# Two layers of a graph network on one core: seven chunks of edges in each layer fetched row by row by SyncE

## The chip, the cores and the metric

The kernel runs on one core of a Trainium2 chip. The metric is the device time of one launch in microseconds (us): three runs of the kernel before took 2022.58 us in the median (2019.66 to 2022.99). The profile is of one more execution, which took 2021.09 us; its span, from the first to the last recorded instruction, is 2019.3 us.

The core's engines are named as in the profile: PE is TensorE's matrix unit and PEld its weight load, DVE is VectorE, ACT is ScalarE, POOL is GpSimd and SP is SyncE, which computes nothing and issues transfers. All transfers, whoever issues them, are carried by the core's 16 DMA engines.

## The reference

There are 6250 nodes with 512 features each and 100000 edges, sorted by destination. Cut to what matters, all in float32:

```python
h = relu(layernorm(x))
norm = -dinv[src] * dinv[dst]              # dinv: degree ** -0.5
prop = lambda v: segment_sum(v[src] * norm[:, None], dst)
h = h @ W1_0 + prop(h) @ W1_1 + b1         # layer 1
h = layer_norm(h, gamma, beta)
h = where(h >= 0, h, 0.01 * h)
out = x + h @ W2_0 + prop(h) @ W2_1 + b2   # layer 2
```

So each layer has two dense products of 6250 x 512 by 512 x 512, and a sum over the edges, for which 100000 rows of 2 KB are read from a table in HBM in the order of `src`.

## The kernel before, in words

*Chunks, units, groups, blocks.* The edges are cut into `NC` = 782 chunks of 128. A chunk is one gather: 128 rows of a table, one in each SBUF partition. Three chunks in a row (`STEP`) form a unit, whose destinations fall into 32 consecutive nodes (`Q`), and four units form a group; there are `NS` = 66 groups in a layer, with up to 12 chunks each. A block is 128 nodes; there are `NB` = 49.

*The gathers.* `gather_to` (L473 to L485) issues them on GpSimd with an indirect DMA each (L480). The rows land in `places`, a tile of 63 places of 528 words per partition: 512 features, and a word D that holds the source's `dinv` in layer 1. Function `slot` (L466) gives a chunk its place. The first chunks fill all 63 places; after that the ring has R = 55 places, and the last eight, R to 62, hold layer 2's weights (`w_late`). GpSimd may run a ring's length ahead of the sums; a gather into a place waits until the sums have read the chunk that lay there. The table of layer 1 (`tab[0]`) has rows of 528 words and that of layer 2 (`tab[1]`) rows of 512. The first 76 chunks (`RAW`) are gathered from x itself before the table is there, and normalized in place (`look_up`, L519). The first 27 chunks of layer 2 are gathered early (`gather_ahead`, L490), before the last three blocks of layer 1 are done; what these lack is added from counts (`count_late`).

*The sums.* For a group, `choose` (L591) makes on VectorE a matrix `sel` of zeros and ones that says which edge belongs to which of the 32 nodes of its unit; in layer 1 `scale` (L635, L647) multiplies it by the word D of the gathered rows, in as few instructions as the places are consecutive. `sums` (L651, L660) multiplies: one matmul for each chunk of the group, 12 in all, unit by unit into 32 rows of `ps`. ScalarE copies the sums to `agg` (L673).

*The dense part.* When all groups of a block are summed, `turn` (L784) collects the block's rows with 0/1 matrices (`place`, L693), and `own`, `first_half`, `second` transpose and multiply by the two weights (L568). `finish` (L746) ends the block. In layer 1 it normalizes and stores the block's rows to layer 2's table (L777) and to `h_tab` (L782); in layer 2 it adds x (L755) and stores the output (L757).

*Order.* The loop over groups (L892) is written out by hand for TensorE, GpSimd and SyncE: they take their instructions in the program's order. VectorE and ScalarE are ordered by a planner. SyncE's queue holds, group by group, the loads of a block's own rows `h` two blocks ahead (L545, two buffers), in layer 2 the loads of x (L564), and the stores. The transfers of SyncE use eight completion semaphores in turn; in the built program a transfer waits for the one eight before it, unless a wait already covers that. Buffers that matter below: `t` has two, `g` one, `xt` two.

*Weights.* W1_1 and W1_0 lie in `w_sb[0]` and `w_sb[1]`, and `w_sb[1]` is last used at the end of layer 1. W2_1 and W2_0 are loaded into `places` in layer 1's group 33 (L896). `pick` and `src_lo` are two small tiles that serve `look_up` and `find` in the first groups and nothing after.

Of the kernel before, what the change touches and what calls it, by code (L numbers as in the profile page):

```python
# [10 lines left out]
BF = mybir.dt.bfloat16  # L11
I32 = mybir.dt.int32
AF = mybir.ActivationFunctionType
OP = mybir.AluOpType
# [11 lines left out]
Q = 32  # L26
# [7 lines left out]
AHEAD_OF = 27  # L34
JOIN = 12


# [6 lines left out]
def gnn_kernel(  # L44
# [85 lines left out]
    sc = const.tile([P, 2, NB], F32, name="sc")  # L130
    pick = const.tile([P, P], BF, name="pick")
    src_lo = const.tile([P, P], BF, name="src_lo")
    src_hi = const.tile([P, RAW], F32, name="src_hi")
# [292 lines left out]
    with tc.If(n_unseen > 0):  # L426
        general_path(tc, x, src, dst, bias1, bias2, gam, bet, w_sb, (W2_1, W2_0), dinv, ndinv, ident, iota_r,
                     eps, out)


def usual_path(tc, have):
    nc = tc.nc
    (x, out, tab, h_tab, ndinv, sidx, dlx, iota_r, w_sb, W2_1, W2_0, w_late, ident, eps, ones, first, nodes_ps, node_of, minus,
     unsorted, dinv, sdinv, bias1, bias2, gam, bet, unseen, unit, N, E, D, NB, NC, NU, NS, KD, rows, places, R,
     load_rest, sc, pick, src_lo, src_hi, eidx, e_src, zero_row, p_id, lent, X) = (
        have[n] for n in ("x out tab h_tab ndinv sidx dlx iota_r w_sb W2_1 W2_0 w_late ident eps ones first nodes_ps node_of "
                          "minus unsorted dinv sdinv bias1 bias2 gam bet unseen unit N E D NB NC NU NS KD rows places "
                          "R load_rest sc pick src_lo src_hi eidx e_src zero_row p_id lent X").split())
    AHEAD = 2
# [11 lines left out]
    with ExitStack() as es:  # L451
# [12 lines left out]
        LATER = places.shape[1] - R  # L464

        def slot(k):  # L466
            return k - X if k < X + R + LATER else (k - X - LATER) % R

        def zr(layer, t):
            k = layer * NC + t  # L470
            return lent[k] if k < X else places[:, slot(k), :D]

        def gather_to(layer, summed_to):  # L473
            nonlocal gathered
            end = summed_to + R
            if layer == 0:
                end = max(end, min(end + LATER, X + LATER + 2 * R))
            for t in range(gathered, min(end, NC)):
                own_scale = layer == 0 and t >= RAW
                nc.gpsimd.indirect_dma_start(  # L480
                    out=places[:, slot(t), :] if own_scale else zr(layer, t), out_offset=None,
                    in_=x if layer == 0 and t < RAW else tab[layer],
                    in_offset=bass.IndirectOffsetOnAxis(
                        ap=lidx[:, t - SHIFTED : t - SHIFTED + 1] if layer and t >= SHIFTED else sidx[:, t : t + 1], axis=0))
            gathered = max(gathered, min(end, NC))  # L485
# [149 lines left out]
        def scale(sel, chunk, of=(0, NQ)):  # L635
# [6 lines left out]
            each = sel.rearrange("p q s e -> p (q s) e")  # L642
            cut = sorted({start, end} | {t for t in range(start + 1, end) if slot(t) != slot(t - 1) + 1})
            for lo, hi in zip(cut, cut[1:]):
                v = each[:, lo - at : hi - at, :]
                k = slot(lo)
                last = nc.vector.tensor_tensor(  # L647
                    v, v, places[:, k : k + hi - lo, D : D + 1].to_broadcast([P, hi - lo, Q]), op=OP.mult)
            return last

        def sums(layer, g, sel, chunk, cnt=None, some=None, opens=True, closes=True):  # L651
# [7 lines left out]
            for s, q in some:  # L659
                nc.tensor.matmul(ps[q * Q : (q + 1) * Q, :], sel[:, q, s, :], zr(layer, chunk[q][s]), start=(s == 0),  # L660
                                 stop=(s == len(chunk[q]) - 1 and (cnt is None or chunk[q][0] >= AHEAD_OF)))
# [224 lines left out]
        for layer in range(2):  # L886
# [5 lines left out]
            for g in range(NS - 1):  # L892
                gather_to(layer, STEP * unit[g])
                if layer == 0 and g == NS // 2:
                    for k, w in enumerate((W2_1, W2_0)):
                        nc.sync.dma_start(w_late[:, k], w.rearrange("(k p) d -> p k d", p=P))  # L896
# [24 lines left out]
                sel, chunk = chosen.pop(g) if g in chosen else choose(g)  # L921
                if layer == 0:
                    with ExitStack() as order:
# [17 lines left out]
                else:  # L941
# [86 lines left out]

def general_path(tc, x, src, dst, bias1, bias2, gam, bet, w_sb, w_late, dinv, ndinv, ident, iota_r, eps,
                 out):  # L1030
# [34 lines left out]
    e_src = dram.tile([NC, P], I32, name="e_src")  # L1065
    e_dst = dram.tile([NC, P], I32, name="e_dst")
    w_sb = list(w_sb)
    for k, w in enumerate(w_late):
# [285 lines left out]
```

## Time and profile before

| | |
|---|---|
| median of three runs | 2022.58 us |
| profiled execution | 2021.09 us |
| its span | 2019.3 us |
| TensorE, matmuls busy | 1669.7 us (83%) |
| GpSimd busy | 1488.9 us (74%) |
| VectorE busy | 707.6 us (35%) |
| ScalarE busy | 414.3 us (21%) |
| mean rate of the DMA engines | 262 GB/s |

A few words on reading it. The slices give the busy share in 40 equal parts of the span, in tenths. A group row has its line, engine, operation and tiles, the count, then busy time and mean duration, then the engine's idle time before these instructions and what ended it. A wait row has the waiting instruction, what released it, the total, the count, and the longest single wait. On GpSimd the recorded duration of a gather is the time in which its descriptors are made, not that in which its data moves; the transfer lands later. "issue" as a releaser means that the engine waited for nothing that the profile shows. SyncE's transfers have their issue time only.

### The profile page before, as it was taken

Reading aid. Unit: us, or ns where it says so; the run is one execution under the profiler, and the core shown is the slowest. Engines: PE = TensorE matmul, PEld = TensorE weight load, DVE = VectorE, ACT = ScalarE, POOL = GpSimd, SP = SyncE. Lnnn points to the kernel's source line nnn. Section 1 sums busy time; section 2 is a strip of 40 time slices with the busy share of each in tenths; the row PEclk is TensorE's granted clock in tenths of the full one; section 3 lists DMA queues with packets and bytes.
Section 4 is the critical chain, followed back from the end, with each engine's and each line's share of the span. In section 5 each row is a group of like instructions: output and inputs, shape, how many; then the busy total and the mean of one; then the engine's idle time right before and its main releaser. Section 6 shows DMA issues by size and latency. Waiting matters only on the chain.

```text
span 2019.3 us, 20097 instructions
## 1 busy us (share of the span) xinstructions
PE 1669.7 (83%) x6907; PEld 669.5 (33%) x6907; DVE 707.6 (35%) x1498; ACT 414.3 (21%) x752; POOL 1488.9 (74%) x1578
## 2 busy tenths in 40 slices
PE   5579998776887776888879888888888888888988
PEld 4444443222333222333323322323332223333333
DVE  7975554333354334343363111112221212222211
ACT  7895221111121111121111010011010001011100
POOL 6477777777777777777777777777777777777774
PEclk8789999888998888989999998889999989989999
DMA  9998888888988888888887787788787878788875
GB/s 329 396 374 269 267 269 263 249 258 245 303 265 253 251 260 241 267 266 260 245 261 241 245 257 247 247 252 255 240 255 246 254 244 257 241 263 251 272 235 171
DMA packets 190131, 528.41 MB, mean 262 GB/s; under 512 B 34652, under 2 KB 36426, under 8 KB 190020
## 3 DMA queue, kind: packets, MB, share of 16 engines
q0 software_dynamic: 125120, 415.88, 67.7%
q1 hardware_dynamic: 64860, 111.14, 15.2%
q8 instruction: 56, 0.92, 0.2%
q14 instruction: 55, 0.45, 0.1%
q10 hardware_dynamic: 40, 0.02, 0.0%
HBM read 475.25 MB, written 51.66 MB: 261 GB/s over the span
## 4 chain that ended last, share of the span: by engine, by line
PE 39%; DMA 31%; POOL 12%; issue 10%; DVE 5%; ACT 2%; POOLq 0%; DVEq 0%; SPq 0%; ACTq 0%
DMA places<-tab,sidx 24%; PE u_ps L568 16%; POOL places L480 12%; PE ps L660 12%; PE an_ps L693 7%; DMA places<-tab,lidx 5%; PE hT_ps L556 1%; PE hT_ps L803 1%; DVE hi L362 1%; DVE lo L362 1%; ACT places L539 1%; DMA dst_c<-in_dst_dram 1%; DMA tab<-places 1%; PE both_ps L379 1%; DVE sel L647 0%
## 5 line engine op out<-in xcount | busy, mean ns | idle before, releaser
L480 POOL DMA_INDIRECT places<-tab,sidx x1191 | 1130.5, 949 | 363.4 <-issue 256.2
L660 PE MATMUL ps<-places,sel 128*32 128x512 f32 x3104 | 517.1, 671 | 145.4 <-DMA places<-tab,sidx 81.9
L693 PE MATMUL an_ps<-agg,there 128*128 128x512 f32 (+1 forms) x554 | 270.0, 620 | 88.2 <-ACT agg L673 83.2
L480 POOL DMA_INDIRECT places<-tab,lidx x270 | 255.3, 946 | 82.3 <-issue 60.9
L660 PEld LDWEIGHTS ps<-places,sel 128*32 128x32 f32 x3104 | 103.1, 117 | 524.1 <-issue 190.0
L607 DVE TENSOR_TENSOR sel<-dlx,nodes_ps 128x384 f32<-128x384 f32 (+3 forms) x134 | 72.4, 541 | 415.1 <-PE ps L660 415.1
L568 PE MATMUL u_ps<-w,hT 128*128 128x512 f32 (+1 forms) x400 | 185.3, 607 | 20.6 <-ACT hT L558 20.1
L673 ACT ACTIVATE agg<-ps 128x512 f32<-128x512 f32 (+2 forms) x130 | 76.1, 587 | 570.1 <-PE ps L660 545.1
L568 PE MATMUL u_ps<-places,hT 128*128 128x512 f32 (+2 forms) x408 | 182.4, 591 | 2.9 <-ACT hT L558 2.9
L568 PE MATMUL u_ps<-w,aT 128*128 128x512 f32 x384 | 173.2, 594 | 2.7 <-DVE aT L805 2.7
L693 PEld LDWEIGHTS an_ps<-agg,there 128*128 128x128 f32 (+1 forms) x554 | 105.8, 199 | 209.6 <-issue 109.8
L568 PE MATMUL u_ps<-places,aT 128*128 128x512 f32 x384 | 173.5, 594 | 0.8 <-DVE aT L805 0.8
L647 DVE TENSOR_TENSOR sel<-sel,places 128x384 f32<-128x384 f32 (+11 forms) x71 | 34.4, 490 | 328.3 <-DMA places<-tab,sidx 323.2
L754 DVE TENSOR_TENSOR u_ps<-u_ps,bias 128x512 f32<-128x512 f32 x45 | 31.5, 700 | 281.8 <-PE u_ps L568 281.8
L558 ACT ACTIVATE hT<-hT_ps 128x512 f32<-128x512 f32 (+1 forms) x98 | 58.2, 594 | 278.1 <-PE hT_ps L556 277.6
L796 ACT ACTIVATE an<-an_ps,ndinv 128x512 f32<-128x512 f32 x96 | 65.8, 685 | 213.7 <-PE an_ps L693 213.5
L681 DVE TENSOR_SCALAR there<-iota_r,node_of 128x128 f32<-128x128 f32 (+1 forms) x286 | 85.8, 302 | 63.6 <-PE an_ps L693 61.3
L568 PEld LDWEIGHTS u_ps<-w,hT 128*128 128x128 f32 (+1 forms) x400 | 73.7, 195 | 96.5 <-issue 74.7
L766 ACT ACTIVATE sd<-mv,eps 128x1 f32<-128x1 f32 (+1 forms) x49 | 14.4, 294 | 433.5 <-DVE mv L764 433.5
L250 POOL DMA_INDIRECT places<-in_x_dram,sidx x63 | 60.0, 952 | 54.0 <-ACT junk L266 21.1
L568 PEld LDWEIGHTS u_ps<-places,hT 128*128 128x128 f32 (+1 forms) x408 | 74.4, 192 | 76.5 <-issue 71.5
L568 PEld LDWEIGHTS u_ps<-w,aT 128*128 128x128 f32 x384 | 70.7, 190 | 83.0 <-issue 77.8
(197 smaller groups left out, 1318.6 us busy)
## 6 DMA issues: line engine op xcount, KB each, us to landing
places<-tab,sidx POOLq DMA_INDIRECT x1191, 3.8
h_tab<-g SPq DMA_DIRECT2D x48, 256.0 KB
xt<-in_x_dram SPq DMA_DIRECT2D x48, 256.0 KB
out_dram<-t SPq DMA_DIRECT2D x48, 256.0 KB
tab<-t SPq DMA_DIRECT2D x46, 256.0 KB
tab<-places SPq DMA_DIRECT2D x22, 528.0 KB
h<-tab SPq DMA_DIRECT2D x45, 256.0 KB
h<-h_tab SPq DMA_DIRECT2D x45, 256.0 KB
```

Source lines behind the costliest of these rows:

```text
L250: nc.gpsimd.indirect_dma_start(out=lent[t] if t < X else places[:, t - X, :D], out_offset=None, in_=x, in_offset=bass.IndirectOffsetOnAxis ...
L362: nc.vector.tensor_tensor(t, s[:, g * 2 * GJ : (g + 1) * 2 * GJ].rearrange("p (j s) -> p j s", s=2)[:, :, None, :] .to_broadcast([EP, GJ, ...
L480: nc.gpsimd.indirect_dma_start(out=places[:, slot(t), :] if own_scale else zr(layer, t), out_offset=None, in_=x if layer == 0 and t < RAW ...
L558: nc.scalar.activation(hT[:, :, :r], ps[:, :, :r], AF.Copy)
L568: nc.tensor.matmul(u_ps[:r], hT[:, kc, :r], w[:, kc, :], start=(start and kc == 0), stop=(stop and kc == KD - 1))
L607: nc.vector.tensor_tensor(sel[:, q : q + k, :w, :], of, node[:, q : q + k, None, :].to_broadcast([P, k, w, Q]), op=OP.is_equal)
L647: last = nc.vector.tensor_tensor(v, v, places[:, k : k + hi - lo, D : D + 1].to_broadcast([P, hi - lo, Q]), op=OP.mult)
L660: nc.tensor.matmul(ps[q * Q : (q + 1) * Q, :], sel[:, q, s, :], zr(layer, chunk[q][s]), start=(s == 0), stop=(s == len(chunk[q]) - 1 and ( ...
L673: nc.scalar.activation(agg[g][: n * Q, lo : lo + w], ps[: n * Q, lo : lo + w], AF.Copy)
L681: behind[1] = nc.vector.tensor_scalar(t[:m, :r], iota_r[:m, :r], node_of[:m, g : g + 1], -(1.0 + i * P), op0=OP.subtract, op1=OP.is_equal)
L693: nc.tensor.matmul(placed[i][:r], t[:m, :r], agg[g][:m, :], start=(g == inside[i][0]), stop=(g == inside[i][-1]))
L796: nc.scalar.activation(an[:r], placed.pop(i)[:r], AF.Copy, scale=ndinv[:r, i : i + 1])
```

## The change

Seven chunks in each layer are no longer gathered by GpSimd. They are 96 apart: the last chunk of every eighth group, from group 15 on in layer 1 and from group 10 on in layer 2 (`ONE_BY_ONE` = (7, 2) are the groups at which the fetching begins). SyncE fetches each of them row by row, with one transfer per edge, whose address in the table is read from SBUF into a register: 16 rows per group, eight ahead of the group's work and eight behind its sums, so a chunk takes eight groups. `fetch` issues eight rows after one register load.

A row is cut into 16 pieces of 32 words, in order that its transfer is shared by 16 engines. In layer 1 each piece is fetched with one word more, 132 bytes, so that the last piece brings the word `dinv` along; in layer 2 a piece has 128 bytes. The pieces land 33 words apart, and the matmul of such a chunk reads 16 x 32 words.

The rows land outside the ring: in layer 1 in places R and R + 1 by turns, in layer 2 in two stretches of `w_sb[1]`. As place R is then in use to the end of layer 1, the load of W2_1 is moved from group 33 to group 64; W2_0 stays. The ring places of the chunks concerned stay empty. The byte addresses are made once, at group 7, in the memory of `pick` and `src_lo` (now one tile): two small loads of `src` and seven instructions of VectorE on seven rows each. The scaling in layer 1 takes the word W - 1 for such a chunk, in an instruction of its own. The general path, which isn't taken with these inputs, loads W1_1 and W1_0 again.

In the built program GpSimd has 699 gathers of layer 1's table instead of 706, and 748 of layer 2's through `gather_to` instead of 755; SyncE has 224 register loads and 1792 row transfers more. TensorE's order is unchanged.

```diff
+AT_ONCE = 8
+PIECES = 16
+ONE_BY_ONE = (7, 2)
+SECOND = 32
...
+        one_by_one, to_fetch = {}, []
+        for layer, g in enumerate(ONE_BY_ONE):
+            each = P // (2 * AT_ONCE)
+            for j, at in enumerate(range(g + each, NS - 2, each)):
+                t = STEP * unit[at + 1] - 1
+                one_by_one[layer * NC + t] = (layer * SECOND + j, R + j % 2 if layer == 0 else j % 2)
+        own_rows = [sorted(k - layer * NC for k in one_by_one if k // NC == layer) for layer in range(2)]
+
+        def set_starts():
...
+                nc.sync.dma_start(starts[rows_of], bass.AP(tensor=src.tensor, offset=src.offset + some[0] * P,
+                                                           ap=[[step * P, n], [1, P]]))
+                nc.vector.tensor_copy(at, starts[rows_of])
+                if layer:
+                    nc.vector.tensor_single_scalar(up, at, float(zero_row), op=OP.is_ge)
+                    nc.vector.tensor_add(at, at, up)
+                nc.vector.tensor_scalar_mul(at, at, 4.0 * tab[layer].shape[1])
+                nc.vector.tensor_copy(starts[rows_of], at)
+
+        PIECE = D // PIECES
+        w_free = w_sb[1].rearrange("p k d -> p (k d)")
+
+        def spread(k):
+
+            at = one_by_one[k][1]
+            row = places[:, at, :] if k < NC else w_free[:, at * W : (at + 1) * W]
+            return row.rearrange("p (a b) -> p a b", a=PIECES)
+
+        def fetch(layer, n=AT_ONCE):
+
+            if not to_fetch:
+                return
+            t, e = to_fetch.pop(0)
+            at = one_by_one[layer * NC + t][0]
...
+            _, regs = nc.values_load_multi_w_load_instructions(
+                starts[at : at + 1, e : e + n], engines=(SP,), min_val=0, max_val=(tab[layer].shape[0] - 1) * tab[layer].shape[1] * 4,
+                skip_runtime_bounds_check_because="rows of the table")
+            flat = tab[layer].bitcast(U8).rearrange("n d -> (n d)")
+            w = PIECE + 1 - layer
+            flat = bass.AP(tensor=flat.tensor, offset=flat.offset, ap=[[1, flat.shape[0]], [PIECE * 4, PIECES], [1, w * 4]])
+            to = spread(layer * NC + t)[:, :, :w].bitcast(U8)
+            for j, start in enumerate(regs):
+                nc.sync.dma_start(to[e + j : e + j + 1], flat[bass.ds(start, 1)])
...
         def zr(layer, t):
             k = layer * NC + t
+            if k in one_by_one:
+                return spread(k)[:, :, :PIECE]
             return lent[k] if k < X else places[:, slot(k), :D]
...
             for t in range(gathered, min(end, NC)):
+                if layer * NC + t in one_by_one:
+                    continue
...
                 if layer == 0 and g == NS // 2:
-                    for k, w in enumerate((W2_1, W2_0)):
-                        nc.sync.dma_start(w_late[:, k], w.rearrange("(k p) d -> p k d", p=P))
+                    nc.sync.dma_start(w_late[:, 1], W2_0.rearrange("(k p) d -> p k d", p=P))
+                if layer == 0 and g == NS - 2:
+                    nc.sync.dma_start(w_late[:, 0], W2_1.rearrange("(k p) d -> p k d", p=P))
...
+                if g == ONE_BY_ONE[layer]:
+                    assert not to_fetch and looked == RAW
+                    if layer == 0:
+                        set_starts()
+                    to_fetch.extend((t, e) for t in own_rows[layer] for e in range(0, P, AT_ONCE))
+                fetch(layer)
                 due = []
...
                     sums(layer, g, sel, chunk, None, step[2], False, True)
+                fetch(layer)
```

More of the change, by code (lines that the diff above doesn't have):

```diff
@@ L130, in gnn_kernel @@
     sc = const.tile([P, 2, NB], F32, name="sc")
-    pick = const.tile([P, P], BF, name="pick")
-    src_lo = const.tile([P, P], BF, name="src_lo")
+    low_of = const.tile([P, 2, P], BF, name="low_of")
+    pick, src_lo = (low_of[:, k, :] for k in range(2))
+    starts = low_of.rearrange("p k e -> p (k e)").bitcast(I32)
     src_hi = const.tile([P, RAW], F32, name="src_hi")
@@ L642, in scale @@
             each = sel.rearrange("p q s e -> p (q s) e")
-            cut = sorted({start, end} | {t for t in range(start + 1, end) if slot(t) != slot(t - 1) + 1})
+            cut = sorted({start, end} | {t for t in range(start + 1, end) if slot(t) != slot(t - 1) + 1
+                                         or t in one_by_one or t - 1 in one_by_one})
             for lo, hi in zip(cut, cut[1:]):
@@ L921, in usual_path @@
                 sel, chunk = chosen.pop(g) if g in chosen else choose(g)
+                assert not any(t in own_rows[layer] and to_fetch and t >= to_fetch[0][0] for c in chunk for t in c)
                 if layer == 0:
```

29 lines of the change are left out of this document (23 added, 6 removed).

## The prediction

> **What bounds the kernel now.** I read the page's head and slices first, then GpSimd's groups and waits, TensorE's waits, the windows, and the timelines of SyncE and of the passage between the layers.
>
> ```profile
> span 2019.3 us, 20097 instructions
> PE 1669.7 (83%) x6907; PEld 669.5 (33%) x6907; DVE 707.6 (35%) x1498; ACT 414.3 (21%) x752; POOL 1488.9 (74%) x1578
> POOL 6477777777777777777777777777777777777774
> DMA  9998888888988888888887787788787878788875
> ```
>
> By busy time TensorE (83%) leads and the DMA engines stand at 8 tenths; POOL's row is a flat 7 from the second slice to the last but one. A flat row is a metronome, so I looked at what a gather costs on GpSimd and what it waits for.
>
> ```profile
> L480 POOL DMA_INDIRECT places<-tab,sidx x1191 | 1130.5, 949 | 363.4 <-issue 256.2 <-DMA places<-tab,sidx 66.7 <-PE ps L660 15.2
> L480 POOL DMA_INDIRECT places<-tab,lidx x270 | 255.3, 946 | 82.3 <-issue 60.9 <-DMA places<-tab,lidx 13.7 <-PE ps L660 3.0
> L490 POOL DMA_INDIRECT places<-tab,eidx x27 | 26.9, 997 | 8.2 <-issue 5.2 <-DMA places<-tab,eidx 1.8 <-DMA h_tab<-g 0.3
> POOL places L480 <- issue: 317.1, 1041, 0.3
> POOL places L480 <- DMA places<-tab,sidx: 66.7, 219, 0.3
> ```
>
> 1488 gathers take 1412.7 us busy and 453.9 us idle, 1866.6 us in all, 1.254 us each. The last number of the two wait rows is the longest single wait: 0.3 us among 1041, and 0.3 us among 219. GpSimd never waits for a buffer, for data or for TensorE; it issues one gather every 0.95 + 0.30 = 1.25 us, and that row of gathers is 92% of the span. TensorE by contrast waits for it:
>
> ```profile
> PE ps L660 <- DMA places<-tab,sidx: 81.9, 64, 3.7
> PE ps L660 <- DMA places<-tab,lidx: 35.2, 23, 3.7
> 700.00:800.00 100.00, 76.06 (x316) 29.37 (x308) 33.53 (x74) 15.96 (x29) 75.73 (x80) 0.89 0.83 253
> 1500.00:1600.00 100.00, 81.35 (x303) 28.36 (x305) 18.59 (x41) 10.01 (x16) 75.73 (x80) 0.95 0.81 250
> 1600.00:1700.00 100.00, 89.92 (x327) 33.63 (x320) 20.93 (x45) 10.60 (x17) 75.66 (x80) 0.93 0.80 247
> ```
>
> The first two rows are TensorE's waits from 1080 to 1980 us, in layer 2: 117 us in which it stood at the sums until a gather landed. The windows (one of layer 1, two of layer 2; columns PE, PEld, DVE, ACT, POOL, granted clock, DMA share, GB/s) have 80 gathers each 100 us. A layer has 66 groups for 782 chunks, 11.85 gathers or 14.8 us a group; of that TensorE is busy 11.3 us (0.76 x 14.8) in the first window, 12.0 in the second and 13.3 in the fullest.
>
> ```profile
> 2000.31 0.95 POOL L480 DMA_INDIRECT places<-tab,lidx  x1 [0.30 <-issue]
> 2003.43 2.77 PE L660 MATMUL ps<-places,sel 128*32 128x512 f32 x12
> ```
>
> Last gather and last sums: after the last gather some 19 us remain, and they don't depend on how many went before.
>
> **The change, part by part.**
>
> *Gathers removed.* GpSimd's program falls from 706 to 699 gathers of layer 1's table, from 755 to 748 of layer 2's: 14. Its order is otherwise the same. 14 x 1.25 = 17.5 us less, if nothing else becomes late. The ring lets GpSimd run 55 places ahead of the sums, so a short delay of TensorE doesn't reach it.
>
> *Rows added on SyncE.* 14 chunks x 128 = 1792 one-row transfers of 16 pieces, and 224 register loads; per group 16 rows and 2 loads. Issue times:
>
> ```profile
> 4.62 0.25 SPq L168 DMA_DIRECT2D src_c<-in_src_dram  x1
> L740 SPq TENSOR_LOAD <-unseen x1: 538/538/538, 2011.6 to 2011.6; - x1
> 702.38 0.32 SPq L777 DMA_DIRECT2D tab<-t  x1
> 703.84 0.32 SPq L782 DMA_DIRECT2D h_tab<-g  x1
> 707.00 0.32 SPq L545 DMA_DIRECT2D h<-tab  x1
> 715.92 0.32 SPq L777 DMA_DIRECT2D tab<-t  x1
> ```
>
> A one-row transfer takes 0.25 us on SyncE, one of 128 rows 0.32. With 0.04 us between two, 16 rows are 4.6 to 5.8 us; two loads 1.1 us; the group's own 2.2 transfers 0.8 us: 6.5 to 7.7 us of 14.8. I take 6.5, as the shape is nearer to one row. The register-held address is not in this trace; the cover is gone at (14.65 - 1.9) / 16 = 0.80 us a row (14.65 us: the mean group with 11.72 gathers).
>
> But issue is not all. SyncE's transfers go through eight completion semaphores in turn, so each waits until the one eight before it has landed. A group's 18.2 transfers are 2.3 rounds of eight, each as long as a landing if that is longer than issuing eight. Bounds from the rows with a landing time (last column, us):
>
> ```profile
> places<-tab,sidx POOLq DMA_INDIRECT x1191, 3.8
> places<-in_x_dram,sidx POOLq DMA_INDIRECT x64, 6.5
> 1016.28 0.32 SPq L777 DMA_DIRECT2D tab<-t  x1
> 1020.54 0.56 DVE L624 TENSOR_TENSOR t<-e_src,iota_r 128x384 bf16<-128x384 f32 x1 [2.92 <-DMA tab<-t]
> ```
>
> 3.8 us is a gather of 128 rows in the main loops, 6.5 us one in the crowded first 120 us; a 256 KB store of SyncE took about 3.9 us (issued by 1016.60, its reader released at 1020.54). SyncE then needs 2.3 x 3.8 + 1.1 = 9.8 us or 2.3 x 6.5 + 1.1 = 16.0 us a group. I take 3.8: the main loops' DMA share is 0.81 to 0.83, as for that row. 9.8 fits into 14.65, so SyncE costs the path nothing. Where it sits: both batches stand between the store of h_tab (703.84) and the next store of the table (715.92), a stretch of 12.1 us that holds only one load of h. Behind a late SyncE queue the loads of h (two blocks ahead), the stores of the table (two buffers of t) and of h_tab (one buffer of g, for which L779 on ScalarE waits) and, in layer 2, the loads of x for the sum at L755; a group's delay of a few us falls into the lead of the loads.
>
> *When the rows are needed.* A chunk's last eight rows are issued after the previous group's sums and are the twelfth operand of the next group's. If they come late, TensorE waits, at most 14 times. A wait of 3.8 us is regained from the 2.8 to 3.5 us that TensorE idles per group: 0 on the path. Without that cover it is 14 x 3.8 = 53 us.
>
> *DMA engines.* The page's queues:
>
> ```profile
> q0 software_dynamic: 125120, 415.88, 67.7%
> q1 hardware_dynamic: 64860, 111.14, 15.2%
> ```
>
> A packet of q1 took on average 15.2% x 2019.3 x 16 / 64860 = 76 ns for 1.7 KB, and q1 moved 22.6 GB/s per engine, by which 132 bytes take 6 ns. Each row gives each engine one small packet and, I assume, one for the completion: 32 a group, 0.2 to 2.4 us of 14.8, so the share goes from 0.83 to between 0.84 and 0.99 (a removed gather gives back 0.01). I take the lower third, 0.88: small packets should be nearer to their bytes than to a 1.7 KB mean. As long as the engines are below 1.0 GpSimd isn't slowed: the windows have one cadence at 0.83 and at 0.80, and its longest wait is 0.3 us. So 0 us. At 80 ns a packet layer 1 would be full.
>
> *Smaller edits.* The scaling at L647 is cut once more in 7 groups, and seven tiny DVE instructions make the addresses at group 7:
>
> ```profile
> L647 DVE TENSOR_TENSOR sel<-sel,places 128x384 f32<-128x384 f32 (+11 forms) x71 | 34.4, 490 | 328.3 <-DMA places<-tab,sidx 323.2
> L896 SPq DMA_DIRECT2D places<-in_L_gnn_W_dram x2: 385/510/636, 537.1 to 537.6; - x2
> 1020.47 0.95 POOL L480 DMA_INDIRECT places<-tab,sidx  x1 [0.30 <-DMA tab<-t]
> 1047.07 0.73 SPq L777 DMA_DIRECT2D tab<-pre  x2
> 1056.87 0.94 POOL L480 DMA_INDIRECT places<-tab,sidx  x1 [0.30 <-issue]
> ```
>
> 14 such DVE instructions at 0.49 us or less are under 7 us, hidden by TensorE's idle time; exposed, under 7. W2_1 (1 MB) leaves 537 us and is put on SyncE two groups before the end of layer 1, ahead of the last three blocks' stores. It takes 1.05 MB / (16 x 22.6 GB/s) = 2.9 us of all engines. The last store of layer 2's table is issued at 1047.07 + 0.73 and lands 3.9 us later at 1051.7; the gather that needs it is issued at 1056.87. The slack is 5.2 us, so 0; the 27 early gathers that make it are kept. Without it, 2.9 us. The matmuls that read rows with a gap every 32 words are 14, unseen here; at the 0.67 us of their group even twice the time is 9 us of TensorE, hidden.
>
> *Sum.* 2019.3 - 17.5 = 2001.8 us of span; 1.8 us lie around it (the profiled run took 2021.1), so 2003.6. The profiled run is 1.5 us under the median of 2022.6, so I say 2005.
>
> **A rule against it.** The Trainium skill (DMA: Bandwidth & Descriptors, section "Issuing engines are not separate DMA queues") says that DMAs of all issuing engines share the 16 engines, and that using several issuers saves only sequencer time, usually small beside the transfer. By that rule nothing is gained and the sum is 2022.6; the trace here disagrees, as issue alone, 1.25 us a gather, is what sets the pace at a DMA share of 0.81.
>
> **The rivals.**
>
> *SyncE becomes the bound (slower).* Place: the 112 groups with rows. It decides when a round of eight lands in over (14.65 - 1.1) / 2.3 = 5.9 us, or a row's issue costs over 0.80 us. At 6.5 us a group is 16.0 us long: 112 x 1.35 = 151, hence 2156 us. For it: 6.5 us is in the trace. Against: only where the DMA share is about 1. Just past the point, at 6.1 us, it is 112 x 0.48 = 54, 2059.
>
> *The DMA engines fill up (slower).* At q0's mean packet (67.7% x 2019.3 x 16 / 125120 = 175 ns) 32 are 5.6 us; 0.83 x 14.8 + 5.6 = 17.9 us against 14.65 in 112 groups: 2369 us; at 90 ns, 0.5 us over in layer 1's 56 groups, 2033. Against: those packets hold 3.3 KB, ours 132 bytes.
>
> *Late rows that TensorE doesn't regain (slower).* 2005 + 53 = 2058. Against it are the idle 2.8 to 3.5 us per group.
>
> *TensorE is the bound already (no change).* GpSimd ends earlier and nothing follows: 2022.6. For it 83% busy and single windows near 90%; against it the 117 us of waits for gathers. If that holds in one layer only, half is gained: 2014.
>
> **How the numbers follow.** Forecast 0.62 (own range 2002 to 2012: 2005 less the 2.9 us by which the lowest of the three runs was under their median, and 2005 with the DVE's 7 us exposed); half the gain 0.05; no change 0.08; SyncE 0.13, engines 0.07, late rows 0.05. About 4 us (0.2%) is what a measurement can tell here. Faster 0.67, same 0.08, slower 0.25. To 2070 the range takes in the late rows and the mild cases of the other two slower rivals and leaves out some 0.15 above and 0.04 below 2000.
>
> **What would show it.** Right: GpSimd's L480 gathers 14 fewer, still 0.95 + 0.30 us with 0.3 as the longest wait; the last gather near 1983 us; SyncE's row issues at 0.25 to 0.32 us; the landing of a gather near 4 us; DMA share under 0.95. Wrong: waits of over 1 us on GpSimd; SyncE waiting on its own rows for most of a group and TensorE waiting at the sums for rows; a DMA share at 1; or GpSimd ending early and TensorE without waits at L660.

## The result and the profile after

The changed kernel took 2048.01 us (median of four runs, 2046.9 to 2049.02), the kernel before on the same chip 2021.99 us (four runs, 2019.66 to 2022.99). The ratio is 1.013, with a 95% interval of 1.0113 to 1.0148: slower by 1.3%, less than 2% but clear of the noise, where 2005 us was forecast. The profiled execution took 2049.02 us, its span is 2047.2 us.

The new lines push the old ones down: the gathers of L480 and L490 are now L543 and L553, TensorE's sums L729 (L660), the scaling L712 (L647), SyncE's loads of h L608 (L545), the stores of the table L846 (L777) and of `h_tab` L851 (L782). The row transfers are L520, their register loads L512.

The page of the kernel after, head, two slice rows and the two queues:

```profile
span 2047.2 us, 24028 instructions
PE 1646.1 (80%) x6907; PEld 679.6 (33%) x6907; DVE 715.2 (35%) x1513; ACT 415.3 (20%) x752; POOL 1476.9 (72%) x1564
POOL 5467777777777777777637777777777777777773
DMA  9998888888888888888748788888888888888884
q0 software_dynamic: 124000, 412.15, 66.1%
q1 hardware_dynamic: 122232, 114.99, 17.5%
```

GpSimd's flat row of sevens now has a dent, 6 and 3, in the middle of the span, and the DMA engines have one there too. Everywhere else the row is as before. GpSimd's groups and its waits say what the dent is:

```profile
L543 POOL DMA_INDIRECT places<-tab,sidx x1179 | 1121.3, 951 | 363.1 <-issue 278.2 <-DMA places<-tab,sidx 37.2 <-PE ps L729 19.7
L543 POOL DMA_INDIRECT places<-tab,lidx x268 | 253.4, 946 | 81.6 <-issue 61.8 <-DMA places<-tab,lidx 10.4 <-PE an_ps L762 3.7
L553 POOL DMA_INDIRECT places<-tab,eidx x27 | 26.0, 963 | 43.1 <-DMA tab<-t 35.1 <-issue 6.1 <-DMA places<-tab,eidx 1.2
POOL places L543 <- issue: 340.0, 1116, 0.3
POOL places L553 <- DMA tab<-t: 35.1, 1, 35.1
```

There are 14 gathers fewer, with the old pace of 0.95 + 0.30 us. But the first of the 27 early gathers of layer 2 waits once, for 35.1 us, until the last needed store of layer 2's table has landed.

The page also follows the chain of work that ended last, from the last instruction back to what released each step. Its shares by engine, before, then after:

```profile
PE 39%; DMA 31%; POOL 12%; issue 10%; DVE 5%; ACT 2%; POOLq 0%; DVEq 0%; SPq 0%; ACTq 0%
PE 47%; SPq 18%; DMA 14%; issue 8%; DVE 6%; POOL 5%; ACT 1%; DVEq 0%; POOLq 0%; ACTq 0%
```

SyncE's issuing (SPq), which was no part of the chain before, is 18% of it now.

The difference of the spans, 2047.2 - 2019.3 = 27.9 us, is made of four pieces. 14 gathers fewer give -17.5. The single wait gives +34.9 (35.15 against 0.30 before). The end gives +7.6: from the start of the last gather to the end of the span it was 19.0 us and is now 26.6 (2020.56 to 2047.2). The first gather of layer 1's table starts at 137.17 instead of 134.92 us, +2.3. Together that is 27.3; 0.6 us stay unaccounted for. GpSimd's stretch from the first early gather to the last gather shortened from 978.6 us (1021.72 to 2000.31) to 969.7 us (1050.82 to 2020.56), which is 8.9 us or seven gathers at 1.25.

What a row costs SyncE stands in the row-issue rows of the trace (duration in ns, least, median and largest, then the first and the last start), and in SyncE's timeline in the middle of layer 1:

```profile
L520 SPq DMA_DIRECT2D places<-tab x896: 506/537/1565, 194.9 to 1030.1; - x180
L512 SPq TENSOR_LOAD <-low_of x224: 518/533/2053, 194.0 to 1934.0; - x112
```

```profile
701.13 10.68 SPq L520 DMA_DIRECT2D places<-tab  x16
711.93 0.51 SPq L608 DMA_DIRECT2D h<-tab  x1
713.16 10.93 SPq L520 DMA_DIRECT2D places<-tab  x16
724.19 0.53 SPq L608 DMA_DIRECT2D h<-tab  x1
724.81 0.38 SPq L846 DMA_DIRECT2D tab<-t  x1
725.28 0.38 SPq L851 DMA_DIRECT2D h_tab<-g  x1
```

A row takes 0.537 us and not 0.25 to 0.32 (0.63 us from one row's start to the next, with the register's move and the gaps), and the transfer right after the rows 0.51 to 0.53 instead of 0.32. From 701.13 to 713.16 one group's rows, two register loads and a load of h fill 12.0 us of the 14.65 us that a group has.

The place of the loss, in SyncE's timeline at the end of layer 1, and then the waits of VectorE, TensorE and GpSimd that belong to it (in brackets the idle time ahead of the instruction, and what ended it):

```profile
1007.34 0.33 SPq L851 DMA_DIRECT2D h_tab<-g  x1
1008.37 22.26 SPq L520 DMA_DIRECT2D places<-tab  x32
1030.73 0.53 SPq L846 DMA_DIRECT2D tab<-t  x1
1031.35 0.38 SPq L851 DMA_DIRECT2D h_tab<-g  x1
1048.06 0.34 SPq L846 DMA_DIRECT2D tab<-t  x1
```

```profile
1032.33 0.19 DVE L712 TENSOR_TENSOR sel<-sel,places 128x32 f32<-128x32 f32 x1 [19.09 <-DMA places<-tab]
1032.58 1.92 PE L729 MATMUL ps<-places,sel 128*32 128x512 f32 x2 [22.62 <-DVE sel L712]
1014.73 0.95 POOL L543 DMA_INDIRECT places<-tab,sidx  x1 [0.30 <-issue]
1050.82 0.94 POOL L553 DMA_INDIRECT places<-tab,eidx  x1 [35.15 <-DMA tab<-t]
```

Read it from the top. The last 32 rows of layer 1's last fetched chunk, the one of group 63, stand in a row in SyncE's queue and take 22 us. VectorE's scaling for that chunk waits 19.09 us until they have landed, and TensorE waits 22.62 us for the scaling. The store of a finished block stands behind the rows (1030.73), and the store of the next block can be made only after group 63's sums (1048.06). GpSimd issued its last gather of layer 1 at 1014.73 and has no work that doesn't need this store until 1050.82. One chunk holds up all three.

Which of the two delays decides is seen at the last needed store. TensorE's start on group 63's sums before, then after, the instruction of VectorE that finishes the store's data, and the first early gather before:

```profile
1000.05 2.78 PE L660 MATMUL ps<-places,sel 128*32 128x512 f32 x24
```

```profile
1007.18 2.78 PE L729 MATMUL ps<-places,sel 128*32 128x512 f32 x22
1047.30 0.73 DVE L843 SCALAR_TENSOR_TENSOR t<-u_ps,dinv,t 128x512 f32<-128x512 f32 x1
```

```profile
1021.72 0.95 POOL L490 DMA_INDIRECT places<-tab,eidx  x1 [0.30 <-DMA h_tab<-g]
```

The data are finished at 1048.03 and the store goes out at 1048.06, so this store doesn't wait in the queue. It is 31.8 us later than before (1016.28, in the prediction's lines), because its data are: TensorE came to group 63's sums 7.1 us late and then stood 22.62 us for the rows.

### The profile page after: what moved, and what is told of

Same layout as the page of the kernel before. It is cut to its first block, busy times and chain, and to the rows that moved or that the text cites. A ratio compares the mean times of both kernels' runs of the same rounds, so it can differ in the third digit from the quotient of the medians.

```text
span 2047.2 us, 24028 instructions
## 1 busy us (share of the span) xinstructions
PE 1646.1 (80%) x6907; PEld 679.6 (33%) x6907; DVE 715.2 (35%) x1513; ACT 415.3 (20%) x752; POOL 1476.9 (72%) x1564
## 3 DMA queue, kind: packets, MB, share of 16 engines
q1 hardware_dynamic: 122232, 114.99, 17.5%
## 4 chain that ended last, share of the span: by engine, by line
PE 47%; SPq 18%; DMA 14%; issue 8%; DVE 6%; POOL 5%; ACT 1%; DVEq 0%; POOLq 0%; ACTq 0%
PE u_ps L631 23%; SPq L520 15%; PE ps L729 12%; PE an_ps L762 7%; POOL places L543 5%; DMA places<-tab,sidx 4%; SPq L512 2%; DMA places<-tab,lidx 2%; PE hT_ps L872 2%; PE hT_ps L619 2%; DMA h<-tab 2%; DMA places<-tab 1%; DMA h_tab<-g 1%; DVE lo L368 1%; DMA h<-h_tab 1%
## 5 line engine op out<-in xcount | busy, mean ns | idle before, releaser
L543 POOL DMA_INDIRECT places<-tab,sidx x1179 | 1121.3, 951 | 363.1 <-issue 278.2
L729 PE MATMUL ps<-places,sel 128*32 128x512 f32 x3090 | 452.6, 633 | 180.9 <-DVE sel L712 70.6
L543 POOL DMA_INDIRECT places<-tab,lidx x268 | 253.4, 946 | 81.6 <-issue 61.8
L729 PEld LDWEIGHTS ps<-places,sel 128*32 128x32 f32 x3090 | 97.8, 112 | 492.7 <-issue 208.1
L762 PE MATMUL an_ps<-agg,there 128*128 128x512 f32 (+1 forms) x554 | 258.1, 600 | 0.1
L631 PE MATMUL u_ps<-w,hT 128*128 128x512 f32 (+1 forms) x400 | 191.3, 623 | 16.3 <-ACT hT L621 8.1
L631 PE MATMUL u_ps<-places,hT 128*128 128x512 f32 (+2 forms) x408 | 189.4, 609 | 3.6 <-DVE t L824 2.2
L631 PE MATMUL u_ps<-w,aT 128*128 128x512 f32 x384 | 185.7, 629 | 1.4 <-DVE aT L874 1.4
L631 PE MATMUL u_ps<-places,aT 128*128 128x512 f32 x384 | 179.3, 610 | 0.8 <-DVE aT L874 0.8
L823 DVE TENSOR_TENSOR u_ps<-u_ps,bias 128x512 f32<-128x512 f32 x45 | 31.5, 700 | 278.3 <-PE u_ps L631 278.3
L829 DVE TENSOR_TENSOR u_ps<-u_ps,bias 128x512 f32<-128x512 f32 x45 | 31.4, 698 | 215.6 <-PE u_ps L631 215.6
L631 PEld LDWEIGHTS u_ps<-places,aT 128*128 128x128 f32 x384 | 73.0, 197 | 84.0 <-issue 82.0
L619 PE MATMUL hT_ps<-ident,h 128*128 128x128 f32 x360 | 59.3, 290 | 47.5 <-DMA h<-tab 33.2
```

What stands on the lines that cost most here:

```text
L543: nc.gpsimd.indirect_dma_start(out=places[:, slot(t), :] if own_scale else zr(layer, t), out_offset=None, in_=x if layer == 0 and t < RAW ...
L619: nc.tensor.transpose(ps[:, kc, :r], h[:r, kc * P : (kc + 1) * P], ident[:r, :r])
L631: nc.tensor.matmul(u_ps[:r], hT[:, kc, :r], w[:, kc, :], start=(start and kc == 0), stop=(stop and kc == KD - 1))
L729: nc.tensor.matmul(to, sel[:, q, s, :], rows_of, start=(s == 0), stop=(s == len(chunk[q]) - 1 and (cnt is None or chunk[q][0] >= AHEAD_OF)))
L762: nc.tensor.matmul(placed[i][:r], t[:m, :r], agg[g][:m, :], start=(g == inside[i][0]), stop=(g == inside[i][-1]))
```

## The experiments

The theory after the result: the loss sits at one place, the end of layer 1, where GpSimd's order ends in gathers that need the last blocks' stores; elsewhere late rows are hidden by the ring, and each gather taken from GpSimd gives its 1.25 us. The rival: rows at 0.54 us on SyncE slow every group a little, and the loss goes with their number. Each measured ratio below is against the kernel before on the same chip, whose median was 2021.51 us for the first four runs, 2022.88 for the next four and 2025.5 for the last three.

**Half the rate.** Eight rows per group, three chunks in each layer:

```diff
-AT_ONCE = 8
+AT_ONCE = 4
```

> Eight rows per group instead of 16 (four per register load), so that a chunk takes 16 groups and only three chunks in each layer are fetched by SyncE; six gathers fewer than before the change instead of 14. Theory (SyncE's queue runs late because 16 rows and two register loads take it some 12 us of a 14.7 us group, and the end of layer 1 waits for that queue): at half the rows SyncE has slack, GpSimd waits 0.3 us at most between the layers, and the time is 2022 - 6 x 1.25 = 2014.5 us. Rival (each small transfer costs a share of the time wherever it stands, by contention on the DMA engines or in SBUF): the loss beside the gain is 43.5 us for 1792 rows, so 768 rows cost 18.6 us, and the time is 2033 us.

2014.45 us, ratio 0.9966 (0.9953 to 0.9978), 7.1 us faster. Six gathers at 1.25 are 7.5. No early gather waits longer than 0.3 us. The rival's 2033 us is out. But the last fetched chunk of layer 1 is that of group 55 here, so this run also takes the rows away from the layer's end, and the rate alone is not tested by it.

**Layer 2 alone, layer 1 alone.** In turn, the list of one layer is empty (and no addresses are made for it, in both runs):

```diff
-            for j, at in enumerate(range(g + each, NS - 2, each)):
+            for j, at in enumerate(range(g + each, NS - 2 if layer else 0, each)):
...
+                if not some:
+                    continue
```

```diff
-            for j, at in enumerate(range(g + each, NS - 2, each)):
+            for j, at in enumerate(range(g + each, 0 if layer else NS - 2, each)):
...
```

> The rows of layer 1 are left to GpSimd again, layer 2's seven chunks stay with SyncE. Theory: the passage between the layers is as in the kernel before (no wait of over 0.3 us on GpSimd's early gathers), the seven gathers of layer 2 give 8.75 us, and the longer tail behind the last gather (26.6 us against 19.0 in the changed kernel) takes 7.6 back: 2021 us, between 2013 and 2024. Rival (cost per row): half of 43.5 less 8.75, so 2035 us.

> The rows of layer 2 are left to GpSimd again, layer 1's seven chunks stay with SyncE. Theory: GpSimd stands some 35 us at the first early gather of layer 2, as in the changed kernel, and the tail is that of the kernel before: 2022 - 8.75 + 35 = 2048 us. Rival (cost per row): 2035 us, with a wait that is shared out.

Layer 2 alone took 2017.41 us, 0.9979 (0.9966 to 0.9991); layer 1 alone 2046.79 us, 1.013 (1.011 to 1.015). GpSimd's waits of layer 1 alone, where these gathers are on L555:

```profile
POOL places L555 <- DMA tab<-t: 34.9, 1, 34.9
```

The wait needs layer 1's rows only: -8.75 + 34.9 = +26.2 us, measured +25.3. Layer 2's rows gave 4.1 us of their 8.75; from the last gather to the end it was 22.3 us there, against 18.0 with layer 1 alone, so some 4 us of it were lost at the very end.

**Stop before the end.** The last two chunks of each layer go back to GpSimd; ten stay with SyncE:

```diff
-            for j, at in enumerate(range(g + each, NS - 2, each)):
+            for j, at in enumerate(range(g + each, NS - 2 - 2 * each, each)):
```

> The last two of the row-by-row chunks in each layer go back to GpSimd, so SyncE's rows end 16 groups earlier; the pace of 16 rows per group stays. Ten gathers fewer than before the change. Theory: SyncE is as late as in the changed kernel in the middle of a layer, but has caught up by its end; the ring hides the delays in the middle: 2022 - 10 x 1.25 = 2009.5 us, GpSimd's first early gather waits 0.3 us, the tail is 19 us. Rival (cost per row): 1280 rows cost 31 us, so 2022 - 12.5 + 31 = 2040 us.

2009.64 us, 0.9938 (0.9919 to 0.9958): 11.9 us faster, ten gathers being 12.5. The same 16 rows a group run through the middle of both layers and cost next to nothing. SyncE's and GpSimd's timelines at the end of layer 1:

```profile
1012.50 0.34 SPq L846 DMA_DIRECT2D tab<-t  x1
```

```profile
1017.93 0.95 POOL L553 DMA_INDIRECT places<-tab,eidx  x1 [0.30 <-issue]
```

The store that was at 1048.06 is at 1012.50. In the kernel after, the gather started 2.8 us after that store's issue; here it starts 5.4 us after it, so the end of layer 1 has some 2.7 us to spare. That is all the slack there is, and the kernel before had the same (1016.28 and 1021.72).

**Why a row costs 0.54 us.** Two things were new in these transfers: an address from a register, and 16 pieces. One kernel keeps the register loads but uses constant addresses (it fetches the first 128 rows of the table each time, so the sums of these chunks are others); one fetches a row in one piece:

```diff
-                nc.sync.dma_start(to[e + j : e + j + 1], flat[bass.ds(start, 1)])
+                nc.sync.dma_start(to[e + j : e + j + 1], flat[(e + j) * 4 * tab[layer].shape[1] : (e + j) * 4 * tab[layer].shape[1] + 1])
```

```diff
-PIECES = 16
+PIECES = 1
...
-                        of = W - 1 if lo in one_by_one else D
+                        of = D
```

> The changed kernel, but a row's address is a constant (rows 0 to 127 of the table) and not a register; the register loads stay. Left out: the 14 chunks are summed from other rows than their edges name, so the output isn't the reference's. If the register address makes a row cost 0.63 us on SyncE instead of the 0.29 us that the prediction took, the row goes to about 0.3 us, SyncE is in time and the time is 2005 us. If the 16 pieces do (descriptors are made at some rate), the row stays at 0.6 us and the time at 2048 us.

> The changed kernel, but a row is fetched as one piece of 2 KB (one word more in layer 1) instead of 16 of 128 bytes. If the pieces set the issue time, a row falls to about 0.3 us, SyncE is in time and the time is about 2005 us, unless the one DMA engine that then carries the rows becomes late (16 rows a group at the 0.11 us that a 2 KB row takes an engine are 1.8 us of 14.7 on an engine that is busy 0.83 of the time: still under 1). If the register address sets it, the row stays at 0.5 to 0.6 us and the time is near 2048 us.

The constant addresses took 2042.7 us, 1.0096 (1.007 to 1.0122), one piece 2016.5 us, 0.9965 (0.9953 to 0.9977). The row-issue rows of the one, then of the other with GpSimd's wait and SyncE's last rows of layer 1:

```profile
L520 SPq DMA_DIRECT2D places<-tab x896: 481/587/1532, 196.9 to 1026.1; - x180
```

```profile
L520 SPq DMA_DIRECT2D places<-tab x896: 227/228/439, 195.7 to 1006.8; - x180
POOL places L553 <- DMA tab<-t: 11.1, 1, 11.1
992.86 14.20 SPq L520 DMA_DIRECT2D places<-tab  x32
```

The register costs nothing; the pieces do, 0.537 against 0.228 us (from one row's start to the next, 0.63 against 0.33; the register load for eight rows took 0.79 us with one piece and 0.53 with 16). With one piece the 32 rows take 14.2 us and not 22.3, and the wait is 11.1 us and not 35.1: -17.5 + 11.1 = -6.4, as measured (2022.88 - 2016.5). So even at the price that the prediction took, the last chunk of layer 1 would still have held up its end.

**The queue alone.** The rows are fetched, but nothing reads them, and all gathers stay on GpSimd, with the places and the scaling of the kernel before:

```diff
         def slot(k):
-            if k in one_by_one:
-                assert k < NC
-                return one_by_one[k][1]
...
         def zr(layer, t):
             k = layer * NC + t
-            if k in one_by_one:
-                return spread(k)[:, :, :PIECE]
...
             for t in range(gathered, min(end, NC)):
-                if layer * NC + t in one_by_one:
-                    continue
...
-                of = W - 1 if lo in one_by_one else D
+                of = D
```

> The rows are fetched as in the changed kernel, but into places that nobody reads, and all gathers are kept, so the sums use those. This is the cost of the rows by themselves. Theory (the loss is the end of layer 1, where the table's stores stand behind the rows in SyncE's queue; and TensorE waiting for rows is a part): no gain of 17.5, the stores are still late, though TensorE doesn't wait for rows: between 2022 and 2065 us, with GpSimd's wait at the first early gather telling how much is the queue alone. If the stores alone make the 35 us, 2057; if TensorE's wait for the rows made SyncE's and the block's lateness, near 2025.

2036.89 us, 1.0062 (1.0043 to 1.0081), +14.0 us. The early gather (here L546), the last needed store (here L838) and TensorE's waits for loads of h:

```profile
POOL places L546 <- DMA tab<-t: 13.8, 1, 13.8
1034.77 0.45 SPq L838 DMA_DIRECT2D tab<-t  x1
```

```profile
PE hT_ps L612 <- DMA h<-tab: 97.1, 12, 12.3
```

The rows delay the stores even where no sum needs them: 13.8 us of wait, which is the whole loss. VectorE finishes this store's data at 1023.38 (L835), so 11.4 us of its lateness are the queue alone, and the data themselves come 7 us after this store's issue in the kernel before, which fits TensorE's waits for late loads of h. Those 97.1 us in total cost nothing beyond that. In the kernel after the same store didn't wait in the queue at all, as shown above: there the wait for group 63's own rows decides. These are two paths side by side of which the longer one counts, so 13.8 us are not a share of the 35.

**W2_1 alone.** The kernel before, with W2_1's load moved to group 64 and nothing else:

```diff
-                    for k, w in enumerate((W2_1, W2_0)):
-                        nc.sync.dma_start(w_late[:, k], w.rearrange("(k p) d -> p k d", p=P))
+                    nc.sync.dma_start(w_late[:, 1], W2_0.rearrange("(k p) d -> p k d", p=P))
+                if layer == 0 and g == NS - 2:
+                    nc.sync.dma_start(w_late[:, 0], W2_1.rearrange("(k p) d -> p k d", p=P))
```

> The kernel before, with nothing changed but the load of W2_1, which moves from group 33 to group 64. The prediction took this at 0 (under 2.9 us): 2022 us. If it holds back the stores of the last blocks, GpSimd waits by that much at the first layer 2 gathers, up to 3 us: 2025 us.

2020.57 us, 0.9984 (0.9972 to 0.9997). The move costs nothing.

**The last chunk alone.** With 16 pieces, only the last chunk of each layer goes back:

```diff
-            for j, at in enumerate(range(g + each, NS - 2, each)):
+            for j, at in enumerate(range(g + each, NS - 2 - each, each)):
```

> Rows of 16 pieces as in the changed kernel, but the last row-by-row chunk of each layer goes back to GpSimd (six in each are left, 12 gathers fewer). If only rows next to the end of the layer hurt: 2022 - 15 = 2007 us, with 0.3 us for GpSimd's first early gather. If SyncE's lateness builds up over the whole layer and isn't worked off in eight groups: a wait of 5 to 20 us is left there, 2012 to 2027 us.

2011.76 us, 0.9925 (0.9898 to 0.9952), 13.7 us faster where twelve gathers are 15.0 (the interval of the ratio leaves 5 us either way). The row issues are still 0.537 us, the longest wait of an early gather is 0.9 us where 0.3 was expected, and from the last gather (1993.44) to the end it is 17.8 us. Group 63's chunk, and in layer 2 group 58's, carry the loss; the other twelve are as good as free at this price of a row. That TensorE is late in the middle of the layer is seen all the same, in its waits before 1060 us, for rows directly or through the scaling:

```profile
PE ps L729 <- DVE sel L712: 48.0, 3, 18.9
PE ps L729 <- DMA places<-tab: 43.8, 3, 18.9
```

These waits, 91.8 us in all, were worked off or covered by the ring before layer 1 ended.

**One piece, without the last chunk of layer 1.** 13 chunks stay with SyncE:

```diff
-PIECES = 16
+PIECES = 1
...
-            for j, at in enumerate(range(g + each, NS - 2, each)):
+            for j, at in enumerate(range(g + each, NS - 2 if layer else NS - 2 - each, each)):
...
-                        of = W - 1 if lo in one_by_one else D
+                        of = D
```

> One piece per row, and the last of layer 1's row-by-row chunks (group 63) goes back to GpSimd; layer 2 keeps its seven. 13 gathers fewer than before the change. Theory (two parts: a row of 16 pieces takes SyncE 0.63 us, and whatever it takes, rows that stand right ahead of the last stores of layer 1 hold these back): the 11.1 us of GpSimd's wait between the layers, which the one-piece rows still had, go, and all 13 gathers count: 2022 - 16.25 = 2006 us. Rival (the one DMA engine that carries the rows is late, and that made the 11 us): as the seven of layer 2 and six of layer 1 stay, some 8 us remain: 2014 us.

2008.34 us, 0.9908 (0.9881 to 0.9935). It has the lowest ratio here and beats both kernels, though its interval overlaps those of stopping early and of the last chunk alone: 17.2 us less than before, with 16.25 worked out for 13 gathers. Its GpSimd passes from layer 1 to layer 2 without a gap:

```profile
1017.48 0.95 POOL L553 DMA_INDIRECT places<-tab,eidx  x1 [0.30 <-issue]
1990.58 0.95 POOL L543 DMA_INDIRECT places<-tab,lidx  x1 [0.30 <-issue]
```

**Four pieces.** The same list with `PIECES = 4` and the scaling of the kernel after. Word W - 1 of a place is not the word `dinv` when there are four pieces, so layer 1's fetched chunks are scaled by another word here; the instructions are the same.

```diff
-PIECES = 16
+PIECES = 4
...
-            for j, at in enumerate(range(g + each, NS - 2, each)):
+            for j, at in enumerate(range(g + each, NS - 2 if layer else NS - 2 - each, each)):
```

> Four pieces of 512 bytes per row, last chunk of layer 1 back to GpSimd, seven in layer 2; 13 gathers fewer. If SyncE's time per row grows evenly with the pieces (0.228 us for one, 0.537 for 16), a row takes 0.29 us here and the time is 2006 us, as with one piece; four DMA engines share the rows instead of one. If it steps up as soon as a row has more than one piece, 0.5 us and 2006 to 2012 us.

2029.04 us, 1.0009 (0.9992 to 1.0025): a miss, for a price between one piece and 16 was expected, and no wait. Its row issues, one wait of GpSimd and one of TensorE:

```profile
L520 SPq DMA_DIRECT2D places<-tab x768: 576/577/776, 192.4 to 908.8; - x192
```

```profile
POOL places L553 <- DMA tab<-t: 9.6, 1, 9.6
```

```profile
PE ps L729 <- DMA places<-tab: 130.6, 6, 25.0
```

Four pieces cost 0.577 us, more than 16. The issue time doesn't grow with the pieces: it is 0.228 us for one and 0.54 to 0.58 for several. TensorE's waits for rows in layer 1 are 130.6 us where the last-chunk run with 16 pieces and the same six chunks of layer 1 had 91.8. In SyncE's timelines its last rows of layer 1 are out by 909.4 us against 897.1, and the store that the early gathers need is issued at 1024.64 instead of 1014.19. So 12 us of lateness at group 54 were regained only in small part in the eleven groups that were left, and the middle of a layer is near its own edge too. That the 0.04 us more a row (0.64 us a group) made this lateness is argued, not shown. Nor is the median explained in full: the trace is of an execution of 2024.04 us, in which the end behind the last gather is 21.9 us long as well; the others took up to 2032.25.

**What stays open.** In the kernel after, SyncE's stores of `h_tab` waited for VectorE, whose planner put the instruction that makes `g` later: in SyncE's waits before, then after,

```profile
SPq L782 <- DVE g L780: 37.9, 36, 2.2
```

```profile
SPq L851 <- DVE g L849: 73.4, 25, 7.1
SPq L851 <- DVE rs L838: 12.4, 1, 12.4
```

Such a wait stands ahead of the rows in the queue and makes them late as well. The one of 12.4 us lies where it matters most: SyncE issued nothing from 979.4 to 991.7 us, and the last 48 rows of layer 1 stood behind that store. A second buffer for `g` would tell how much of the 35 us that is; it wasn't tried. In the version with one piece and 13 chunks such waits reach 20.3 us and do no harm, but there no rows stand at the end of layer 1.

## Why the prediction was wrong

*The bound and the gain were right.* GpSimd's pace of 1.25 us a gather sets the time. Layer 2 shortened by 8.9 us for seven gathers, and runs without a wait at the end of layer 1 gave 7.1 us for 6 gathers, 11.9 for 10, 13.7 for 12 and 17.2 for 13, against 7.5, 12.5, 15.0 and 16.25 worked out (layer 2 alone, late at its own end, gave 4.1 of 8.75). The rule of the Trainium skill (DMA: Bandwidth & Descriptors, section "Issuing engines are not separate DMA queues") that more issuers save only issue time, usually little, which by the prediction's words would leave the time at 2022.6, is not borne out here: 13 gathers moved with one-piece rows gave a ratio of 0.9908.

*The step that failed first: "A one-row transfer takes 0.25 us on SyncE, one of 128 rows 0.32 ... I take 6.5" of a group's 14.65 us.* Both ends came from transfers of other shapes, and the measured 0.537 us lies outside them. One group's queue is 12.0 us. The price of a row that isn't in the trace was bounded from two sides by rows that shared nothing with it but the engine; the term was mis-sized by a factor of two. The register load (0.533 us, 0.538 taken) was right.

*The step that failed and decided: "SyncE costs the path nothing" and "0 on the path" for late rows.* That reasoning took the mean group: 9.8 us of 14.65, and TensorE's 2.8 to 3.5 us of idle time per group to regain a delay (by its own fullest window it is 1.5). It holds where a next group follows, as the runs that stop early show. TensorE's waits for rows were also longer than the 3.8 us taken: it waited seven times in layer 1, 117.8 us in all, and up to 22.6 at once. The reasoning doesn't hold at group 63, behind which only two groups of layer 1 are left: there a delay goes straight into the stores, and from these into GpSimd. For W2_1 the prediction did work out a slack near this place, 5.2 us, at the last store of the table; at the first early gather it is 2.7. It didn't ask the same of the rows that stand in the same queue ahead of the same stores. With 16 pieces that cost 34.9 us; with a row at 0.228 us, near the assumed price, the wait was still 11.1 and the time 2016.5.

*The rivals.* "Late rows that TensorE doesn't regain" gave 2058 and the mild case of "SyncE becomes the bound" 2059; the time was 2048. Neither mechanism was it as priced: the late rows cost 35 us once and not 3.8 us 14 times, and SyncE's queue stayed under the threshold of 0.80 us a row, though it was 18% of the chain that ended last. The range of 2000 to 2070 held the time because it was drawn wide enough for them, which is no merit of the forecast.

*The end.* "Some 19 us remain, and they don't depend on how many went before" was wrong by 7.6 us. TensorE's timeline of the kernel after has the last sums 10.2 us after the start of the last gather (2020.56), where it was 3.1 us before:

```profile
2030.76 2.77 PE L729 MATMUL ps<-places,sel 128*32 128x512 f32 x12
```

So TensorE was still 7 us behind GpSimd. That this comes from the rows of group 58's chunk fits the run that gave the last chunk of each layer back, in which the end is 17.8 us.

*The DMA engines* were bounded rightly. A row made 32 packets more, as assumed ((122232 - 64860) / 1792 = 32.0). They took 14 ns each (17.5% of 2047.2 us less 15.2% of 2019.3 us, times 16, over 57372 packets). The windows of the kernel after show shares of 0.86 and 0.84 where 0.88 was taken, with GpSimd's 80 and 81 gathers per 100 us as before:

```profile
700.00:800.00 100.00, 72.59 (x289) 29.14 (x288) 37.98 (x90) 16.53 (x30) 75.93 (x80) 0.86 0.86 256
1500.00:1600.00 100.00, 80.41 (x293) 31.14 (x288) 19.01 (x41) 9.56 (x16) 75.64 (x81) 0.90 0.84 255
```

The wait for the transfer eight before, on which the prediction spent its middle value of 9.8 us, didn't bind: the rows went out back to back. With one piece it did bind in part: in that trace SyncE's waits ahead of rows for the landing of its stores of `h_tab` are 37.4 us in 29 waits, the longest 2.4. W2_1's move cost 0, as forecast. Not foreseen was a wait of 4.2 us, in which GpSimd waited for TensorE ahead of layer 1's first table gather; the 2.3 us at the start come from it.

## What to carry to other kernels

A delay that a ring or a double buffer hides in the middle of a loop can be paid in full at the loop's end, where the last results release the next stage: work out the slack of every moved instruction at that place, not for the mean group. On an engine that takes its instructions in order, the rows in front of a critical store can hold it up by as much as their issue takes, even where nobody needs them (here 11.4 us behind 22.4 us of rows). Take bulk work off such a queue before the last groups, and price a transfer of a new shape by a run, since its neighbours in the trace didn't bound it.

## What the runs showed of the hardware

- The issue time of a single row on SyncE depended on whether its pattern had one piece or several: 0.228 us for one of 2 KB, 0.577 for four of 512 bytes, 0.537 for 16 of 128 or 132 bytes. The count of pieces as such doesn't set it, as 128 rows of 2 KB took 0.32. A constant address in place of the register made it no cheaper (0.587 against 0.537). Why several pieces of one row cost more is open.
- A row in n pieces made 2 n packets: 2.0 with one piece, 8.0 with four, 32.0 with 16. The Trainium skill (DMA: Bandwidth & Descriptors, section "Why a DMA increments its semaphore by 16 and not by 1") says that the size of the slowest dimension sets how many engines share a transfer, so that 16 pieces go to 16 engines; the counts agree with that, taking one packet and one completion for each engine. It adds that software can split a contiguous row so that it is spread over them. Here that was the dear choice: the split made each row's issue 2.4 times as long, and the version with the lowest ratio doesn't share.
- A small packet, completions counted, took 14 ns of one DMA engine (worked out above from the two pages): nearer to the 6 ns that the prediction works out for 132 bytes than to the 76 ns of the queue's mean packet.
